# Column logits by a VectorE turn and DMA, chunked first weights, and a recalibrated schedule in a four-layer graph network

## The chip, the cores and the metric

The kernel runs on one core of a Trainium2 chip. The metric is the device time of one execution in microseconds, and the kernel before takes 3336.84 us, the median of three runs (3336.81 to 3337.57). The engines are named as in the profile: PE is TensorE's matrix multiplication and PEld its weight load, DVE is VectorE, ACT is ScalarE, POOL is GpSimd, and SP is the engine whose queue issues every DMA of this kernel.

## The reference, cut to what matters

There are 128 batches, each a graph of 128 nodes with 512 features in float32, and one adjacency matrix for all of them. Four layers follow one another, each with a residual sum and a layer norm:

```python
x = ln(x + (adj @ x) @ W0 + bias0)                        # layer 0
h = x @ W                                                 # layer 1
s1, s2 = h @ a1, h @ a2
e = leaky_relu(s1[:, :, None] + s2[:, None, :], 0.2) * adj
h_prime = softmax(e, axis=2) @ h
x = ln(x + elu(h_prime + beta * h))
x = ln(x + max over n of relu(adj @ x + ...))             # layer 2, a maximum
qkv = x @ w_qkv                                           # layer 3: 8 heads of 64
attn = softmax(where(adj == 0, -inf, q @ k.T * scale))
o = (attn @ v) @ w_proj + b_proj
x = ln(x + o + ln(o) * gamma + beta)
```

In layer 1 the logit of nodes n and m is the sum of a row logit `s1[n]` and a column logit `s2[m]`. The row logits stand one per partition, as a column of a tile. The column logits are wanted along the free axis, the same in every partition, so they have to be turned.

## The kernel before, in words

Every batch is a tile x of 128 partitions (nodes) by 512 features that stays in on-chip memory from its load to its store; there are 16 such buffers. Two batches form a group (`G = 2`). A batch's chain of work is the generator `batch(i)`. Layer 0 mixes nodes with the transposed adjacency (`mixed`, L207) and multiplies by W0 (`product`, L199). The logits s1 and s2 are two reductions on DVE against `wa_rows` (L548), which are W times a1 and a2. For the group's two batches together, `attention1` forms the logits' matrix, the softmax and its transposed form eT, with a round trip through DRAM (`e_d`). Layer 1 mixes with eT, multiplies by W (L199), and applies the ELU on ACT and DVE (L564 to L567). Layer 2 is one matmul (L575), a maximum (L578) and a bias on ACT. Layer 3 turns x by 32x32 blocks on DVE and a round trip through DRAM (`x_d`, to the tile xT), makes queries and keys for the group (`query_key`, L451), values (`values`), the scores (L604), the softmax (L611 to L629), its turn through DRAM (`p_d`, to the tile prT), the weighted sum (`attend`, L480) and the projection (L199 again), with the last two layer norms on DVE. A float32 matmul of the program is two instructions in the trace, a transpose on PE is one.

In `attention1` before, the column logits are turned on PE: L392 transposes a broadcast of the column s2 against the identity, once for each batch of the pair, into a `tr` bank of PSUM, where all partitions then hold s2 along the free axis. L396 reads it from PSUM, in the order of 32-node blocks that the later turn wants, and adds s1 of the partition, twice, into z. L403 to L409 make the leaky maximum, the product with the adjacency and the negated row maximum.

The order of instructions on every engine is written by a planner at build time. `Plan` holds the time at which each engine and each buffer comes free. A chain asks for an engine with `use(engine, work, buffers, late, urgent)`: `work` is how long the engine is held, `late` how long after that the result is there. The request with the earliest start is issued next; among equal starts, urgent ones go first, then the lower rank, which is the batch number. Requests of PE start `MARGIN`, 1.0 us, after their operands. Each engine then runs its instructions strictly in that order, and waits where an operand is late. DMAs are requests on SP, and `landing` estimates when the first loads land. The last six batches have ranks lowered by 12, so that they go ahead of those before them. The buffers that matter here are three PSUM banks `tr`, three `mm`, and 16 buffers x. A buffer is asked for where its name stands in `use`, and `give` frees it.

Work on PE takes these costs in the plan: 3.5 for each product and each query-key block, 0.98 for a mixing, 0.95 for layer 2, 1.1 for scores, 0.25 and 0.9 for each batch's weighted sum, and 0.3 for the logits' transposes.

Of the kernel before, what the change touches and what calls it, by code (L numbers as in the profile page):

```python
# [8 lines left out]
F32 = mybir.dt.float32  # L9
# [6 lines left out]
P = 128  # L16
# [13 lines left out]
    "tr": 3, "mm": 3, "sc": 1,  # L30
    "x": 16, "yT": 3, "e": 2, "et": 1, "eT": 2, "ex": 2, "xT": 2, "v": 8, "qkT": 3,
    "pr": 2, "pt": 1, "xt": 2, "prT": 2, "oT": 2, "o": 2,
# [10 lines left out]
class Plan:  # L43
# [46 lines left out]
    def at(self, r):  # L90
        engine, _, take, _, _ = r["want"]
        t = max(r["ready"] + (MARGIN if engine == "PE" else 0.0), self.free.get(engine, 0.0))
        names = take()
        for n, name in enumerate(names):
            i = (self.next[name] + names[:n].count(name)) % BUFS[name]
            t = max(t, self.slots[name][i])
        return t
# [21 lines left out]
def gnn_stack_kernel(  # L119
# [41 lines left out]
    def mean_rstd(src):  # L161

        yield use("DVE", 1.0)
        st = small.tile([P, 6], F32, name="st")
        nc.vector.bn_stats(st, src)  # L165
        mv = small.tile([P, 2], F32, name="mv")
        nc.vector.bn_aggr(mv, st)  # L167
        ve = small.tile([P, 1], F32, name="ve")
        nc.vector.tensor_scalar(ve, mv[:, 1:2], EPS, None, op0=ALU.add)  # L169
        yield use("POOL", 0.65, late=0.1, urgent=True)  # L170
        rstd = small.tile([P, 1], F32, name="rstd")
        nc.gpsimd.tensor_tensor(rstd, ve, neghalf, op=ALU.pow)  # L172
        return mv, rstd
# [14 lines left out]
    def pool_add(dst, other, event, after=None):  # L188
        if after:
            yield after  # L190
        yield use("POOL", 1.35)
        nc.gpsimd.tensor_tensor(dst, dst, other, op=ALU.add)  # L192
        done(event)
# [8 lines left out]
    def mixed(xb, nodes):  # L202

        b0, b1 = yield use("PE", 0.98, lambda: ("tr", "yT"), late=0.2)
        p = bank([P, K, P], "tr")
        for k in range(K):
            nc.tensor.matmul(p[:, k, :], xb[:, k * P : (k + 1) * P], nodes, start=True, stop=True)  # L207
# [39 lines left out]
    loaded = [Event() for _ in range(NB)]  # L247
    adj_in, adj_ready, w0_in, bias0_in, w1_in = (Event() for _ in range(5))
    scalars_in, w3_in, wa_ready = (Event() for _ in range(3))
# [7 lines left out]
    def load(i):  # L257
        x_slot[i] = yield use("SP", 0.1, "x")
        xs[i] = buf([P, D], "x")
        nc.sync.dma_start(xs[i], x[i])  # L260
        landing(loaded[i], P)
# [4 lines left out]
    def loads():  # L266
# [3 lines left out]
        yield from load(0)  # L270
        yield use("SP", 0.4)
        matrix(w0_sb, w0)
        landing(w0_in, K * P)
        yield from load(1)
# [32 lines left out]

    def adjacency():
        yield adj_in
        b0 = yield use("PE", 0.3, "tr", late=0.2, urgent=True)  # L310
# [41 lines left out]
    class Group:  # L352


        def __init__(self):
            self.s = small.tile([P, G, 2], F32, name="s")
            self.logits = [Event(2) for _ in range(G // 2)]
            self.attention = [Event() for _ in range(G // 2)]
            self.turned, self.qk = Event(G), Event(K)
            self.rows, self.attended = ([Event() for _ in range(G)] for _ in range(2))  # L360
            self.heads, self.o = {}, {}
            self.eT, self.xT, self.qkT, self.slot, self.left = {}, None, None, {}, {}
# [9 lines left out]
    def group(g):  # L372
        if g not in groups:
            groups[g] = Group()
            for h in range(G // 2):
                plan.start(attention1(groups[g], h), g * G + 2 * h - (12 if g * G >= NB - 6 else 0))
            for n in range(K):
                plan.start(query_key(groups[g], n // 2 * 2 + K * (n % 2)), g * G + n / K - (12 if g * G >= NB - 6 else 0))

            for bs in ((0, 1),) if g * G < NB - G else ((0,), (1,)):  # L380
                plan.start(attend(groups[g], bs), g * G - (12 if g * G >= NB - 6 else 0))
        return groups[g]


    def attention1(gr, h):
        yield gr.logits[h]
        yield scalars_in
        s = gr.s
        b0 = yield use("PE", 0.3, "tr", late=0.2, urgent=True)
        p = bank([P, 2, P], "tr")  # L390
        for i in range(2):
            nc.tensor.transpose(p[:, i, :], s[:, 2 * h + i, 1:2].to_broadcast([P, P]), ident)  # L392
        be = yield use("DVE", 2.1, "e", urgent=True)
        z = one.tile([P, 2, P], F32, name="z")
        for i in range(2):
            nc.vector.tensor_scalar(  # L396
                z[:, i, :].rearrange("p (c r) -> p c r", c=Q),
                p[:, i, :].rearrange("p (r c) -> p c r", c=Q),
                s[:, 2 * h + i, 0:1], None, op0=ALU.add,
            )  # L400
        give(b0)
        e = buf([P, 2, P], "e")
        nc.vector.scalar_tensor_tensor(e, z, ALPHA, z, op0=ALU.mult, op1=ALU.max)  # L403
        nc.vector.tensor_tensor(
            e, e, adj_cols.rearrange("p c r -> p (c r)")[:, None, :].to_broadcast([P, 2, P]),
# [22 lines left out]
        scratch = dram.tile([P, Q, 2 * S], F32, name="e_d")  # L428
        yield use("SP", 0.1, late=2.0)
        to_rows(et.rearrange("p c i s -> p c (i s)"), scratch)  # L430
        give(bt)
        gr.slot[h] = yield use("SP", 0.1, "eT", late=2.6)
        eT = buf([P, Q, 2 * S], "eT")
# [5 lines left out]
    def query_key(gr, c):  # L439
        yield gr.turned  # L440
        yield w3_in
        got = yield use("PE", 3.5, lambda: ("mm",) if gr.qkT else ("mm", "qkT"), late=0.2)
        if gr.qkT is None:
# [24 lines left out]
    def attend(gr, bs):  # L468
        for b in bs:
            yield gr.rows[b]  # L470
        slots = yield use(
            "PE", 0.25 + 0.9 * len(bs), lambda: ("tr", "oT") * len(bs), late=0.2, urgent=True
        )
# [17 lines left out]
    def values(i, gr, event):  # L491
        b = i % G
        yield gr.turned
        bp = yield use("PE", 3.5, "mm", late=0.2)
        p = product(
# [10 lines left out]
    def features(xt, bt, gr, b):  # L506

        scratch = dram.tile([P, Q, P], F32, name="x_d", bufs=8)
        yield use("SP", 0.1, late=2.3)
        to_rows(xt, scratch)  # L510
# [13 lines left out]
    def batch(i):  # L524
# [9 lines left out]
        plan.start(pool_add(xb, bias0_sb, biased, bias0_in), i)  # L534
        yield w0_in
        bp = yield use("PE", 3.5, "mm", late=0.2)
        p = product(lambda k: yT[:, k, :], lambda k: w0_sb[:, k, :])
# [6 lines left out]
        yield wa_ready  # L544
        yield use("DVE", 1.6)
        for j in range(2):
# [10 lines left out]
        gr.read(h, 2)  # L557
        bp = yield use("PE", 3.5, "mm", late=0.2)
        p = product(lambda k: yT[:, k, :], lambda k: w1_sb[:, k, :])
# [4 lines left out]
        nc.scalar.activation(ex, p, AF.Exp)  # L564
        yield use("DVE", 1.5, urgent=True)
        nc.vector.scalar_tensor_tensor(xb, p, 0.0, xb, op0=ALU.max, op1=ALU.add)  # L566
# [8 lines left out]
        nc.tensor.matmul(p, adjT, xb, start=True, stop=True)  # L575
# [9 lines left out]

        bt = yield use("DVE", 0.65, "xt")
        xt = buf([P, Q, P], "xt")
# [9 lines left out]

        bs = yield use("PE", 1.1, "sc", late=0.2, urgent=True)
        sc = bank([P, 2, K, P], "sc")
# [54 lines left out]

        bp = yield use("PE", 3.5, "mm", late=0.2)
        p = product(lambda k: oT[:, k, :], lambda k: wproj_sb[:, k, :])
# [9 lines left out]
        yield added  # L666
        yield use("DVE", 1.65)
        t1 = one.tile([P, D], F32, name="t1")
# [5 lines left out]
        yield from layernorm_dve(xb)  # L674
        yield use("SP", 0.1, late=3.0)
        nc.sync.dma_start(out[i], xb)
        give(x_slot[i])

    with tc.manual_schedule(
# [4 lines left out]
        for i in range(NB):  # L684

            plan.start(batch(i), i if i < NB - 6 else i - 12)
        plan.run()
# [27 lines left out]
```

## Time and profile before

| what | value |
|---|---|
| median of three runs | 3336.84 us |
| the profiled execution | 3337.14 us, span 3335.1 us |
| PE busy | 3303.4 us, 99% of the span |
| DVE busy | 2662.2 us, 80% |
| ACT, POOL busy | 1185.1 us (36%), 922.5 us (28%) |
| granted TensorE clock, mean | 0.998 |
| DMA | 296 MB, mean 89 GB/s |

The profile is of one execution. Its own time is 2.0 us over its span, and 0.3 us over the median of the runs. In the rows of groups the columns are: line, engine, operation, what is written and read, shapes, count, then busy us and mean ns of one, then the idle time of the engine just before them and what ended most of it. The names of tiles stand without numbers, so `w_sb` is the weight of layer 0 or of layer 1, `mm` a PSUM bank. PE's matmuls overlap in the array, and so the mean of one (594 ns for 512 columns) is longer than the distance of one start from the next.

### The profile page before, as it was taken

The page shows a single profiled execution, that of the slowest core. Times are in us where ns is not written, and L with a number is a line of the kernel's source. Part 1 is how long each engine was busy: PE and PEld are TensorE (multiplying, and loading weights), DVE is VectorE, ACT ScalarE, POOL GpSimd, SP SyncE. Part 2 cuts the span into 40 slices and gives each one's busy share as a digit, 9 for nine tenths or more (in the row PEclk, how much of TensorE's full clock was granted, in tenths as well). Part 3 has the DMA queues.
Part 4 walks back from the last instruction along what each step waited for, and adds up shares of the span by engine and source line. Part 5 has one row for each costly group of instructions (what it writes and reads, how often), then busy time and mean ns, then how long its engine had stood idle before and what let it go on. Part 6 is the DMA issues. An engine that isn't in the chain of part 4 may idle for free.

```text
span 3335.1 us, 43586 instructions
## 1 busy us (share of the span) xinstructions
PE 3303.4 (99%) x14729; PEld 2069.6 (62%) x14729; DVE 2662.2 (80%) x5527; ACT 1185.1 (36%) x3457; POOL 922.5 (28%) x1031
## 2 busy tenths in 40 slices
PE   9999999999999999999999999999999999999998
PEld 5666666566656666656566666556666656656655
DVE  7878779877878778877986877987787877887786
ACT  3433333333334343333343333234233333334332
POOL 2222223222232322312331322412232232332232
PEclk9999999999999999999999999999999999999999
DMA  4322322232222222232223223223322223222232
GB/s 159 100 97 69 98 89 59 97 99 92 86 89 71 91 92 86 77 107 82 74 82 113 81 83 89 83 89 83 111 79 86 73 94 97 72 86 81 74 105 78
DMA packets 458190, 296.00 MB, mean 89 GB/s; under 512 B 315888, under 2 KB 389744, under 8 KB 457968
## 3 DMA queue, kind: packets, MB, share of 16 engines
q1 hardware_dynamic: 457968, 293.23, 28.9%
q8 instruction: 117, 1.92, 0.2%
q14 instruction: 105, 0.86, 0.1%
HBM read 150.54 MB, written 142.61 MB: 88 GB/s over the span
## 4 chain that ended last, share of the span: by engine, by line
PE 87%; DVE 11%; DMA 1%; issue 1%; SPq 0%; ACT 0%; POOL 0%; POOLq 0%; DVEq 0%
PE mm L199 45%; PE mm L451 25%; PE tr L207 5%; PE sc L604 4%; PE tr L480 3%; PE mm L575 3%; DVE st L165 2%; DVE scr L548 1%; DVE x L186 1%; DVE x L541 1%; DVE mv L167 1%; DVE xt L588 1%; DVE x L672 0%; DVE mx L578 0%; DVE x L567 0%
## 5 line engine op out<-in xcount | busy, mean ns | idle before, releaser
L199 PE MATMUL mm<-w_sb,yT 128*128 128x512 f32 x2048 | 910.7, 594 | 1.7 <-DVE x L566 1.2
L451 PE MATMUL mm<-xT,wqkv_sb 128*128 128x256 f32 x4096 | 908.0, 380 | 1.0 <-DVE mx L578 1.0
L451 PEld LDWEIGHTS mm<-xT,wqkv_sb 128*128 128x128 f32 x4096 | 772.5, 190 | 130.1 <-issue 18.8
L172 POOL TENSOR_TENSOR rstd<-ve,neghalf 128x1 f32<-128x1 f32 x640 | 407.6, 637 | 1461.7 <-DVE ve L169 1232.8
L199 PEld LDWEIGHTS mm<-w_sb,yT 128*128 128x128 f32 x2048 | 381.0, 190 | 444.9 <-issue 431.3
L199 PE MATMUL mm<-wqkv_sb,xT 128*128 128x512 f32 x1024 | 464.3, 596 | 0.0
L622 ACT ACTIVATE pr<-pr,nmx 128x128 f32<-128x128 f32 x1024 | 397.7, 391 | 170.0 <-DVE nmx L618 168.6
L199 PE MATMUL mm<-wproj_sb,oT 128*128 128x512 f32 x1024 | 457.0, 595 | 0.0
L192 POOL TENSOR_TENSOR x<-x,o 128x512 f32<-128x512 f32 x128 | 177.2, 1385 | 659.9 <-DVE o L660 658.0
L165 DVE BATCH_NORM_STATS2 st<-x 128x6 f32<-128x512 f32 x512 | 349.0, 682 | 8.1 <-ACT x L582 7.3
L199 PEld LDWEIGHTS mm<-wproj_sb,oT 128*128 128x128 f32 x1024 | 192.6, 191 | 226.2 <-issue 222.9
L181 ACT ACTIVATE x<-x,nmr,rstd 128x512 f32<-128x512 f32 x256 | 205.1, 810 | 338.7 <-DVE nmr L179 314.2
L199 PEld LDWEIGHTS mm<-wqkv_sb,xT 128*128 128x128 f32 x1024 | 188.4, 190 | 197.4 <-issue 190.7
L611 DVE TENSOR_TENSOR pr<-sc,maskb 128x1024 f32<-128x1024 f32 x128 | 156.0, 1219 | 189.6 <-PE sc L604 189.5
L210 ACT COPY yT<-tr 128x512 f32<-128x512 f32 x256 | 147.9, 583 | 232.6 <-PE tr L207 232.2
L192 POOL TENSOR_TENSOR x<-x,bias_sb 128x512 f32<-128x512 f32 x128 | 178.4, 1402 | 129.4 <-PE tr L207 121.3
L192 POOL TENSOR_TENSOR x<-x,beta_sb 128x512 f32<-128x512 f32 x128 | 167.3, 1309 | 157.5 <-DVE xt L588 142.0
L548 DVE SCALAR_TENSOR_TENSOR scr<-x,wa_rows 128x512 f32<-128x512 f32 x256 | 192.2, 751 | 17.8 <-ACT x L181 11.9
L459 ACT ACTIVATE qkT<-mm 128x512 f32<-128x512 f32 x128 | 76.0, 593 | 339.0 <-PE mm L451 338.8
L622 ACT ACTIVATION_READ_ACCUMULATOR pr<-pr,nmx 128x1 f32 x1024 | 193.3, 189 | 0.0
L500 ACT COPY v<-mm 128x512 f32<-128x512 f32 x128 | 74.8, 585 | 333.0 <-PE mm L199 333.0
L186 DVE TENSOR_SCALAR x<-x,mv,rstd 128x512 f32<-128x512 f32 x256 | 168.1, 661 | 14.4 <-POOL rstd L172 14.3
(63 smaller groups left out, 3551.2 us busy)
## 6 DMA issues: line engine op xcount, KB each, us to landing
p_d<-pt SPq DMA_DIRECT2D x128, 512.0 KB, 2.6
prT<-p_d SPq DMA_DIRECT2D x128, 512.0 KB, 3.8
x<-in_x SPq DMA_DIRECT2D x128, 256.0 KB, 2.7
x_d<-xt SPq DMA_DIRECT2D x128, 256.0 KB, 2.0
xT<-x_d SPq DMA_DIRECT2D x512, 64.0 KB, 2.4
out<-x SPq DMA_DIRECT2D x128, 256.0 KB, 2.0
e_d<-et SPq DMA_DIRECT2D x64, 128.0 KB, 1.7
eT<-e_d SPq DMA_DIRECT2D x64, 128.0 KB, 2.2
```

The lines of the kernel that those rows point to most:

```text
L165: nc.vector.bn_stats(st, src)
L172: nc.gpsimd.tensor_tensor(rstd, ve, neghalf, op=ALU.pow)
L181: nc.scalar.activation(xb, xb, AF.Identity, bias=nmr, scale=rstd)
L186: nc.vector.tensor_scalar(xb, xb, mv[:, 0:1], rstd, op0=ALU.subtract, op1=ALU.mult)
L192: nc.gpsimd.tensor_tensor(dst, dst, other, op=ALU.add)
L199: nc.tensor.matmul(p, lhs(k), rhs(k), start=(k == 0), stop=(k == K - 1))
L207: nc.tensor.matmul(p[:, k, :], xb[:, k * P : (k + 1) * P], nodes, start=True, stop=True)
L210: nc.scalar.copy(yT, p)
L451: nc.tensor.matmul(p[:, j, :], wqkv_sb[:, k, (c + j) * P : (c + j + 1) * P], gr.xT[:, k, :], start=(k == 0), stop=(k == K - 1),)
L548: nc.vector.scalar_tensor_tensor(scr, xb, 1.0, wa_rows[:, j, :], op0=ALU.mult, op1=ALU.mult, accum_out=gr.s[:, b, j : j + 1],)
L611: nc.vector.tensor_tensor(pr, sc.rearrange("p j c m -> p (j c) m"), maskb[:, None, :].to_broadcast([P, H, P]), op=ALU.add,)
L622: nc.scalar.activation(pr[:, j, :], pr[:, j, :], AF.Exp, bias=nmx[:, j : j + 1], accum_out=sums[:, j : j + 1],)
```

## The change

The column logits no longer go through PE. DVE turns a broadcast of s2 by 32x32 blocks into the small tile s2 (64 elements per partition, both batches of the pair). One DMA writes four partitions of it, one of each block of 32 nodes, to DRAM (`s_d`) in the order of 32-node blocks that z has, and a second reads that row of 256 numbers into all 128 partitions of the tile z. One addition of 128x256 on DVE then adds s1. The reads wait on SP's queue for the write's landing.

The first weights come as four DMAs of 128 rows instead of one, and batch 0's first product is planned on the second chunk. Twelve transposes of the identity stand on PE ahead of the adjacency's transpose; nothing reads them. `MARGIN` counts for a request only in proportion to its ready time up to 20 us of plan. Many planned durations change; the ELU's second step and layer 2's second step on DVE become requests of their own, and their PSUM banks are given free before them. The last eight batches have ranks lowered by 8, instead of the last six by 12. The scratch rows p_d have eight buffers instead of four, and a group takes both its prT buffers at once.

```diff
-    "x": 16, "yT": 3, "e": 2, "et": 1, "eT": 2, "ex": 2, "xT": 2, "v": 8, "qkT": 3,
+    "x": 16, "yT": 3, "z": 2, "e": 2, "et": 1, "eT": 2, "ex": 2, "xT": 2, "v": 8, "qkT": 3,
...
-        t = max(r["ready"] + (MARGIN if engine == "PE" else 0.0), self.free.get(engine, 0.0))
+        t = max(r["ready"] + (min(MARGIN, r["ready"] / 20) if engine == "PE" else 0.0), self.free.get(engine, 0.0))
...
-        yield use("DVE", 1.0)
+        yield use("DVE", 1.03)
         st = small.tile([P, 6], F32, name="st")
...
-        yield use("POOL", 1.35)
+        yield use("POOL", 1.4)
         nc.gpsimd.tensor_tensor(dst, dst, other, op=ALU.add)
...
-        b0, b1 = yield use("PE", 0.98, lambda: ("tr", "yT"), late=0.2)
+        b0, b1 = yield use("PE", 0.91, lambda: ("tr", "yT"), late=0.2)
...
-        x_slot[i] = yield use("SP", 0.1, "x")
+        x_slot[i] = yield use("SP", 0.5, "x")
...
-        yield use("SP", 0.4)
-        matrix(w0_sb, w0)
-        landing(w0_in, K * P)
+        for k in range(K):
+            yield use("SP", 0.4)
+            nc.sync.dma_start(w0_sb[:, k, :], w0[k * P : (k + 1) * P])
+            landing(w0_chunk[k], P)
         yield from load(1)
...
     def adjacency():
+
+        b0 = yield use("PE", 2.5, "tr")
+        p = bank([P, K, P], "tr")
+        for i in range(12):
+            nc.tensor.transpose(p[:, i % K, :], ident, ident)
+        give(b0)
         yield adj_in
...
-                plan.start(attention1(groups[g], h), g * G + 2 * h - (12 if g * G >= NB - 6 else 0))
+                plan.start(attention1(groups[g], h), g * G + 2 * h - (8 if g * G >= NB - 8 else 0))
...
         s = gr.s
-        b0 = yield use("PE", 0.3, "tr", late=0.2, urgent=True)
-        p = bank([P, 2, P], "tr")
-        for i in range(2):
-            nc.tensor.transpose(p[:, i, :], s[:, 2 * h + i, 1:2].to_broadcast([P, P]), ident)
+
+        yield use("DVE", 0.2)
+        st = small.tile([P, 2, Q, S // Q], F32, name="s2")
+        nc.vector.transpose(
+            st.rearrange("p i c u -> p i u c"),
+            s[:, 2 * h : 2 * h + 2, 1:2, None].to_broadcast([P, 2, S // Q, Q]),
+        )
+        row = dram.tile([2 * Q, Q, S // Q], F32, name="s_d")
+        yield use("SP", 0.5, late=2.0)
+        nc.sync.dma_start(
+            row.rearrange("j a u -> a j u"), st[::S].rearrange("p i c u -> p (i c) u")
+        )
+        bz = yield use("SP", 0.5, "z", late=2.2)
+        z = buf([P, 2, P], "z")
+        nc.sync.dma_start(
+            z, row.rearrange("j a u -> (j a u)")[None, :].to_broadcast([P, 2 * P]).rearrange(
+                "p (i f) -> p i f", i=2
+            ),
+        )
         be = yield use("DVE", 2.1, "e", urgent=True)
-        z = one.tile([P, 2, P], F32, name="z")
-        for i in range(2):
-            nc.vector.tensor_scalar(
-                z[:, i, :].rearrange("p (c r) -> p c r", c=Q),
-                p[:, i, :].rearrange("p (r c) -> p c r", c=Q),
-                s[:, 2 * h + i, 0:1], None, op0=ALU.add,
-            )
-        give(b0)
+        nc.vector.tensor_tensor(
+            z, z, s[:, 2 * h : 2 * h + 2, 0:1].to_broadcast([P, 2, P]), op=ALU.add
+        )
         e = buf([P, 2, P], "e")
         nc.vector.scalar_tensor_tensor(e, z, ALPHA, z, op0=ALU.mult, op1=ALU.max)
+        give(bz)
...
-        got = yield use("PE", 3.5, lambda: ("mm",) if gr.qkT else ("mm", "qkT"), late=0.2)
+        got = yield use("PE", 3.46, lambda: ("mm",) if gr.qkT else ("mm", "qkT"), late=0.2)
...
-        yield w0_in
-        bp = yield use("PE", 3.5, "mm", late=0.2)
+        yield w0_chunk[1]
+        bp = yield use("PE", 3.46, "mm", late=0.2)
...
-        yield use("DVE", 1.6)
+        yield use("DVE", 1.7)
         for j in range(2):
...
-        yield use("DVE", 1.5, urgent=True)
+        yield use("DVE", 0.69, urgent=True)
         nc.vector.scalar_tensor_tensor(xb, p, 0.0, xb, op0=ALU.max, op1=ALU.add)
+        give(bp)
+        yield use("DVE", 0.8)
         nc.vector.scalar_tensor_tensor(xb, ex, 1.0, xb, op0=ALU.min, op1=ALU.add)
-        give(bp)
         give(be)
...
-        bp = yield use("PE", 0.95, "mm", late=0.2, urgent=True)
+        bp = yield use("PE", 0.88, "mm", late=0.2, urgent=True)
...
-        yield use("DVE", 0.89, urgent=True)
+        yield use("DVE", 0.69, urgent=True)
         mx = small.tile([P, 1], F32, name="mx")
         nc.vector.tensor_reduce(mx, p, axis=AX.X, op=ALU.max)
+        give(bp)
+        yield use("DVE", 0.21)
         nc.vector.tensor_scalar(mx, mx, b2_sb, 0.0, op0=ALU.add, op1=ALU.max)
-        give(bp)
...
-        bs = yield use("PE", 1.1, "sc", late=0.2, urgent=True)
+        bs = yield use("PE", 1.13, "sc", late=0.2, urgent=True)
...
-        scratch = dram.tile([P, Q, H * S], F32, name="p_d")
-        yield use("SP", 0.1, late=2.8)
+        scratch = dram.tile([P, Q, H * S], F32, name="p_d", bufs=8)
+        yield use("SP", 0.5, late=2.8)
         to_rows(pt.rearrange("p c h s -> p c (h s)"), scratch)
         give(bt)
-        bt = yield use("SP", 0.1, "prT", late=4.0)
+        got = yield use("SP", 0.5, lambda: () if gr.prT else ("prT",) * G, late=4.0)
+        gr.prT = gr.prT or got
+        bt = gr.prT.pop()
...
-        yield use("DVE", 1.65)
+        yield use("DVE", 1.9)
         t1 = one.tile([P, D], F32, name="t1")
...
-            plan.start(batch(i), i if i < NB - 6 else i - 12)
+            plan.start(batch(i), i if i < NB - 8 else i - 8)
```

More of the change, by code (lines that the diff above doesn't have):

```diff
@@ L247, in gnn_stack_kernel @@
     loaded = [Event() for _ in range(NB)]
-    adj_in, adj_ready, w0_in, bias0_in, w1_in = (Event() for _ in range(5))
+    adj_in, adj_ready, bias0_in, w1_in = (Event() for _ in range(4))
+    w0_chunk = [Event() for _ in range(K)]
     scalars_in, w3_in, wa_ready = (Event() for _ in range(3))
@@ L360, in __init__ @@
             self.rows, self.attended = ([Event() for _ in range(G)] for _ in range(2))
-            self.heads, self.o = {}, {}
+            self.heads, self.o, self.prT = {}, {}, []
             self.eT, self.xT, self.qkT, self.slot, self.left = {}, None, None, {}, {}
@@ L375, in group @@
             for h in range(G // 2):
-                plan.start(attention1(groups[g], h), g * G + 2 * h - (12 if g * G >= NB - 6 else 0))
+                plan.start(attention1(groups[g], h), g * G + 2 * h - (8 if g * G >= NB - 8 else 0))
             for n in range(K):
-                plan.start(query_key(groups[g], n // 2 * 2 + K * (n % 2)), g * G + n / K - (12 if g * G >= NB - 6 else 0))
+                plan.start(query_key(groups[g], n // 2 * 2 + K * (n % 2)), g * G + n / K - (8 if g * G >= NB - 8 else 0))
             for bs in ((0, 1),) if g * G < NB - G else ((0,), (1,)):
-                plan.start(attend(groups[g], bs), g * G - (12 if g * G >= NB - 6 else 0))
+                plan.start(attend(groups[g], bs), g * G - (8 if g * G >= NB - 8 else 0))
         return groups[g]
@@ L428, in attention1 @@
         scratch = dram.tile([P, Q, 2 * S], F32, name="e_d")
-        yield use("SP", 0.1, late=2.0)
+        yield use("SP", 0.5, late=2.0)
         to_rows(et.rearrange("p c i s -> p c (i s)"), scratch)
         give(bt)
-        gr.slot[h] = yield use("SP", 0.1, "eT", late=2.6)
+        gr.slot[h] = yield use("SP", 0.5, "eT", late=2.6)
         eT = buf([P, Q, 2 * S], "eT")
@@ L471, in attend @@
         slots = yield use(
-            "PE", 0.25 + 0.9 * len(bs), lambda: ("tr", "oT") * len(bs), late=0.2, urgent=True
+            "PE", 0.25 + 0.88 * len(bs), lambda: ("tr", "oT") * len(bs), late=0.2, urgent=True
         )
@@ L508, in features @@
         scratch = dram.tile([P, Q, P], F32, name="x_d", bufs=8)
-        yield use("SP", 0.1, late=2.3)
+        yield use("SP", 0.5, late=2.3)
         to_rows(xt, scratch)
@@ L534, in batch @@
         plan.start(pool_add(xb, bias0_sb, biased, bias0_in), i)
-        yield w0_in
-        bp = yield use("PE", 3.5, "mm", late=0.2)
+        yield w0_chunk[1]
+        bp = yield use("PE", 3.46, "mm", late=0.2)
         p = product(lambda k: yT[:, k, :], lambda k: w0_sb[:, k, :])
@@ L557, in batch @@
         gr.read(h, 2)
-        bp = yield use("PE", 3.5, "mm", late=0.2)
+        bp = yield use("PE", 3.46, "mm", late=0.2)
         p = product(lambda k: yT[:, k, :], lambda k: w1_sb[:, k, :])
@@ L583, in batch @@
         yield from layernorm_dve(xb)
-        bt = yield use("DVE", 0.65, "xt")
+        bt = yield use("DVE", 0.71, "xt")
         xt = buf([P, Q, P], "xt")
@@ L653, in batch @@
         give(ba)
-        bp = yield use("PE", 3.5, "mm", late=0.2)
+        bp = yield use("PE", 3.46, "mm", late=0.2)
         p = product(lambda k: oT[:, k, :], lambda k: wproj_sb[:, k, :])
@@ L674, in batch @@
         yield from layernorm_dve(xb)
-        yield use("SP", 0.1, late=3.0)
+        yield use("SP", 0.5, late=3.0)
         nc.sync.dma_start(out[i], xb)
```

## The prediction

> **What bounds the kernel now.** I read the page first: busy time, then the groups by line with shapes kept apart, then PE's waits, then the chain and the timeline at both ends.
>
> ```profile
> span 3335.1 us, 43586 instructions
> ...
> PE 3303.4 (99%) x14729; PEld 2069.6 (62%) x14729; DVE 2662.2 (80%) x5527; ACT 1185.1 (36%) x3457; POOL 922.5 (28%) x1031
> ```
>
> TensorE (PE) is busy 99% of the span and is idle for 3335.1 - 3303.4 = 31.7 us in all. The next engine, VectorE (DVE), has a fifth of its time free. So a change gains only by taking instructions off PE or by closing PE's 31.7 us. The waits of PE say where those are (columns: total us, times, longest):
>
> ```profile
> PE tr L392 <- DVE scr L548: 6.2, 8, 1.2
> PE tr L480 <- DMA prT<-p_d: 4.4, 2, 4.1
> PE tr L207 <- DMA x<-in_x: 3.3, 2, 2.3
> PE tr L312 <- DMA adj_sb<-in_adj: 2.6, 1, 2.6
> PE mm L575 <- ACT x L181: 1.4, 2, 0.7
> PE mm L199 <- DVE x L566: 1.2, 1, 1.2
> ```
>
> The largest is in front of the very transposes that the change removes. About 10 us more lie after the last matmul. The chain of waits gives PE's pace:
>
> ```profile
> 70.11 0.22 PE tr L392 x2
> ```
> ```profile
> 283.87 0.32 PE tr L392
> ```
> ```profile
> 3213.22 17.17 PE mm L199 x40
> ```
>
> The two logit transposes of a pair of batches take 0.22 us when nothing is late, 0.11 each; 40 matmuls of 512 columns take 17.17, so a product of eight takes 3.43. The piece at 283.87 is one transpose that had waited for the logits' reductions on DVE. PE's timeline at the start and at the end:
>
> ```profile
> 4.10 2.04 PE L207 MATMUL tr<-adjT,x 128*128 128x128 f32 x8 [1.02 <-DMA x<-in_x]
> 8.41 2.07 PE L207 MATMUL tr<-adjT,x 128*128 128x128 f32 x8 [2.27 <-DMA x<-in_x]
> 10.28 7.68 PE L199 MATMUL mm<-w_sb,yT 128*128 128x512 f32 x16
> ```
> ```profile
> 3309.03 1.09 PE L480 MATMUL tr<-prT,v 128*64 128x128 f32 x16
> 3314.26 1.97 PE L480 MATMUL tr<-prT,v 128*64 128x128 f32 x16 [4.13 <-DMA prT<-p_d]
> 3316.16 8.57 PE L199 MATMUL mm<-wproj_sb,oT 128*128 128x512 f32 x16
> ```
>
> At the start, the first product stands behind the mixing of batch 1, which waits for that batch's x. At the end the attention of the last batch waits 4.1 us for its DMA, while the projection of the batch before, whose operand was copied at 3310.8, stands behind it; after that idle time the granted clock is 0.59 (windows of 5 us, 3315 to 3320), and 16 matmuls take 8.57 us instead of 6.9.
>
> **The change part by part**, against the profiled execution: span 3335.1, with 2.0 around it 3337.1; the median of the runs, 3336.8, is 0.3 lower.
>
> *Transposes off PE.* 64 pairs of 0.22 us: -14.1 us. All of it is on the path, since PE is the bound there.
>
> *The wait in front of them.* PE's idle time there is 6.2 us by the waits, PEld's 9.7; counted from matmul start to matmul start in the trace, the places at L392 hold 9.4 us more than 0.11 for each. It goes, but DVE was late there, and the next matmul fed by DVE may wait instead. At 283.87 independent matmuls follow for 6.9 us, so most of it does not come back: bounds 0 and -9.4, I take -7.5.
>
> *What VectorE gets instead.*
>
> ```profile
> L396 DVE TENSOR_SCALAR z<-tr,s 128x128 f32<-128x128 f32 x128 | 38.5, 342 | 3.1 <-PE tr L392 3.0
> L404 DVE TENSOR_TENSOR e<-e,adj_cols 128x256 f32<-128x256 f32 x64 | 31.0, 484 | 2.2
> L426 DVE STREAM_TRANSPOSE et<-e 128x128 f32<-128x128 f32 x128 | 39.9, 311 | 5.1 <-DMA e_d<-et 0.8
> ```
>
> Two adds from PSUM go (38.5 us in all). One add of 128x256 comes, like L404, 0.48, and one block transpose of 128x64, between the smallest DVE operation (0.15, L169) and L426's 0.31: I take 0.22, from its half size. 64 x 0.70 = 45 us, so DVE gains 6 us of work and stays at 80%: nothing on PE's path.
>
> *Two more DMAs per pair on SP's queue.* Nearest rows, in us to landing:
>
> ```profile
> e_d<-et SPq DMA_DIRECT2D x64, 128.0 KB, 1.7
> eT<-e_d SPq DMA_DIRECT2D x64, 128.0 KB, 2.2
> ```
>
> Their issues take 0.33 and 0.37, so 128 more cost SP's queue about 45 us of 3335, beside everything else. Round trip: 1.7 + 2.2 = 3.9, up to 3.2 + 3.9 = 7.1 by the longest of each. The plan allows 0.5 + 2.0 + 0.5 + 2.2 = 5.2, so there is 1.3 us of slack, and PE's requests are planned 1.0 us behind their operands besides. The new wait is of DVE: the add at the head of a pair's 2.1 us of work. Behind it stand evacuations of PSUM (L541, L566, L660) for which PE waits by the three mm banks. On SP, the read holds whatever is queued behind it (x loads, p_d, x_d) until the write has landed, as p_d does now (265.5 us in 112 waits of SP). Bounds 0 and +54 us (below, the second rival); nearest are the medians: +1. The batch's longer latency is covered by 16 x buffers, 16 x 26 us of work.
>
> *First weights in chunks, dummy transposes.* w0 lands at 1.65 + 6.04 = 7.7 and the first product starts at 10.28. With chunks it is planned on the second chunk and hence ahead of batch 1's mixing. The dummies start when the identity is there (1.3) and take 12 x 0.22 (the mixing's pace at the start) = 2.6, to 3.95; adjacency's transpose 0.44 and copy 0.29, mixing to 6.6, its copy 0.59: product at 7.3. At full pace it ends at 10.8, and with batch 1's mixing and product at 15.5 to 16, against 17.79 now. If the array stays slow until 11.6, as it does now (from there the trace's clock record is 1.0), five matmuls take 0.85 each (start to start of the first product's first ones now) and the second product ends near 17.3. Bounds -3 and +1 (the dummies delay adjacency by 1.3); I take -1.5. The four issues of 0.43 move x1, bias and w1 back by 1.3 us on SP, behind 327 GB/s of transfers in the first 20 us, which is what they land by.
>
> The Trainium skill, "TensorE: Matmul & The Clock Gate", Part 4 on PE-mode transposes, says that transposes do not count as activity that raises the clock. By it the dummies would raise nothing, the start would bring 0.5 and the sum would be 3311; no run here shows it yet.
>
> *Calibrated plan.* From the planner's costs a batch asked 26.2 us of PE before (4 products and 2 query-key blocks at 3.5, two mixings at 0.98, 0.95, 1.1, about 1.2 for the rest) and 25.6 now; the chain shows 25.3. So PE ran ahead of the plan, relative to DVE, whose costs rise (a batch from 22.1 to 22.8; busy 20.8). Other waits of PE in mid-kernel sum to some 5 to 6 us from start to start (L575, L451 and L199 behind ACT and DVE). A truer plan should close some; a new order can open others: bounds -6 and +8, I take -2. SP's 0.5 for 0.1 (0.33 to 0.37 measured) moves requests apart in the plan; SP's planned 5.5 us per batch stay far under 25. Twice the p_d buffers and the paired prT cost nothing: SP's waits name no p_d reader, and attention frees both prT at once now.
>
> *Last eight ahead by 8 instead of six by 12.* It changes the filler work behind the last softmax. The order named above costs 4.1 idle and 1.7 of slow clock. Best -8 (both, and some of the 10 us after the last matmul), worst +8 (less filler: the last softmax to prT takes 3296.3 to 3314.1, and 12.2 of these 17.8 us are filled now). I take -3, half of what the misplaced projection costs.
>
> Sum: -14.1 - 7.5 + 1 - 1.5 - 2 - 3 = -27.1: 3310.0, by the median's offset 3309.7, rounded 3310.
>
> The skill's "VectorE: DVE Perf Modes", Rules for kernel authors, gives 128x128 transposes to TensorE where PSUM will do. That speaks against the change: by it nothing is gained and the time stays near 3337. The rule takes PE to have room, and this trace has PE at 99% against DVE at 80%.
>
> **Rivals.**
> 1. *The waits only move.* DVE was late, not the transposes; the next matmul pays, and ends and plan bring nothing net: 3337.1 - 14.1 and the start's 1.5 = 3321.5. For it: PEld waits 4.7 us in 9 places at L575 behind ACT too. Against it: independent matmuls follow.
> 2. *The logits' round trip holds VectorE* (slower). If each takes the longest rows, 7.1, DVE waits 1.9 beyond the plan, 0.9 beyond PE's margin, 64 x 0.85 = 54 us: 3310 + 54 = 3364. It decides from 0.4 us of PE wait per pair, a round trip of 6.6. Against it: medians of 3.9.
> 3. *The rebuilt order gives it back*: the plan's and the tail's worst bounds, +8 and +8, in place of -2 and -3, and 4 us of waits at the round trip: 3310 + 10 + 11 + 4 = 3335, no change. For it: the tail's filler is tight. Against it: PE's pace in the plan comes nearer to the chain's.
> 4. *Everything closes*: -14.1 - 9.4 - 3 - 6 - 8 = 3296.5, about 3297.
>
> **How the numbers follow.** Forecast 0.62 (3300 to 3320), rival 1 0.19, rival 2 0.07, rival 3 0.06, rival 4 0.06. 0.2% or 6.7 us is about what a measurement of this kernel tells from no change. Faster: 0.62 + 0.19 + 0.06 = 0.87; same 0.06; slower 0.07. The range 3299 to 3328 takes in rival 1 with some of a bad tail and leaves out rivals 2 and 3 and most of 4, nearly 0.2.
>
> **What would show it.** L392 gone and PE with 128 fewer matmuls; span down by 14 plus what PE's idle time falls, from 31.7 to about 19; DVE's idle in front of the new add under 10 us in total (rival 2: over 50); the first product at 7 to 8 us, at a pace that tells whether the dummies raised the clock; the last two projections not behind a wait of 4 us. The prediction is wrong if PE's idle grows at L575, L207 (eT) or L480, or if the tail after 3300 is longer.

## The result, and the profile after

The changed kernel takes 3312.35 us, the median of four runs (3311.0 to 3316.2), against 3337.03 before: a ratio of 0.9928, with a 95% interval of 0.9910 to 0.9945. The forecast was 3310. The total was right. Four of the six terms it was summed from were not: the wait and the plan by errors that cancel, the start and the tail. The experiments below show it.

The page of the changed kernel, its span and its first line of busy times:

```profile
span 3309.2 us, 43603 instructions
...
PE 3286.0 (99%) x14613; PEld 2060.0 (62%) x14613; DVE 2640.0 (80%) x5527; ACT 1182.6 (36%) x3457; POOL 935.1 (28%) x1031
```

The span is 25.9 us shorter. PE has 116 matmuls fewer: the 128 logit transposes are gone and the twelve dummies have come. PE is idle for 3309.2 - 3286.0 = 23.2 us instead of 31.7; 19 was forecast. DVE is no busier than before.

The windows view cuts the span into the start, the middle and the end. Its columns are: the stretch and its length, then busy us and instructions of PE, PEld, DVE, ACT and POOL, then granted clock, DMA share and GB/s. First the kernel before, then the one after:

```profile
0.00:60.00 60.00, 51.98 (x200) 30.73 (x201) 42.69 (x108) 15.11 (x29) 21.50 (x26) 1.00 0.58 211
60.00:3050.00 2990.00, 2980.81 (x13294) 1867.83 (x13293) 2407.32 (x5014) 1078.35 (x3143) 831.45 (x928) 1.00 0.29 86
3050.00:3336.00 286.00, 270.57 (x1237) 171.09 (x1235) 212.15 (x406) 91.66 (x286) 69.58 (x79) 0.98 0.28 86
```
```profile
0.00:60.00 60.00, 57.58 (x222) 33.93 (x223) 42.51 (x102) 15.86 (x29) 23.43 (x27) 1.00 0.56 207
60.00:3050.00 2990.00, 2987.25 (x13301) 1877.10 (x13300) 2406.11 (x5067) 1082.65 (x3158) 845.83 (x931) 1.00 0.30 90
3050.00:3310.00 260.00, 241.19 (x1094) 148.97 (x1092) 191.36 (x360) 84.13 (x271) 65.83 (x73) 0.97 0.29 89
```

Length less busy time is PE's idle time, the last stretch taken to the end of the span:

| stretch | before | after |
|---|---|---|
| 0 to 60 us | 8.0 | 2.4 |
| 60 to 3050 us | 9.2 | 2.8 |
| 3050 us to the end | 14.5 | 18.0 |

The middle and the start gained, the end lost. In the start, 2.8 us of the busy time after are the dummies, which do no work. Counted from matmul starts at the pace of full clock, PE has done its first 40 us of real work at 52 us before and at 47 after, so the start gains about 5 us.

PE's waits of the changed kernel (total us, times, longest; line numbers have moved, so attention is L499 here and layer 2 is L595):

```profile
PE tr L499 <- DMA prT<-p_d: 4.6, 1, 4.6
PE mm L595 <- ACT x L181: 2.1, 1, 2.1
PE mm L199 <- ACT yT L210: 2.0, 2, 1.4
PE mm L199 <- ACT oT L675: 1.5, 2, 0.7
```

The wait behind the logits' reductions (6.2) is gone. The wait for the last prT (4.4 before) is still there: it is the same wait one batch earlier, as PE's timeline at the end shows:

```profile
3272.60 1.16 PE L625 MATMUL sc<-qkT 64*128 64x128 f32 x16
3273.69 7.13 PE L199 MATMUL mm<-wproj_sb,oT 128*128 128x512 f32 x16
3285.42 1.44 PE L499 MATMUL tr<-prT,v 128*64 128x128 f32 x16 [4.60 <-DMA prT<-p_d]
3287.59 6.30 PE L199 MATMUL mm<-wproj_sb,oT 128*128 128x512 f32 x8 [0.73 <-ACT oT L675]
3293.82 1.09 PE L499 MATMUL tr<-prT,v 128*64 128x128 f32 x16
3295.66 3.70 PE L199 MATMUL mm<-wproj_sb,oT 128*128 128x512 f32 x8 [0.74 <-ACT oT L675]
```

The last two batches now go in the order attention, projection, attention, projection, so no projection stands behind another batch's wait. But PE runs out of work at 3280.8, waits at the attention of the last batch but one, and the eight matmuls after that take 6.3 us instead of 3.7; the trace's clock record is 0.5 from 3286.0 to 3292.9.

### The profile page after: what moved, and what is told of

Same layout as the page of the kernel before. It is cut to its first block, busy times and chain, and to the rows that moved or that the text cites. A ratio compares the mean times of both kernels' runs of the same rounds, so it can differ in the third digit from the quotient of the medians.

```text
span 3309.2 us, 43603 instructions
## 1 busy us (share of the span) xinstructions
PE 3286.0 (99%) x14613; PEld 2060.0 (62%) x14613; DVE 2640.0 (80%) x5527; ACT 1182.6 (36%) x3457; POOL 935.1 (28%) x1031
## 4 chain that ended last, share of the span: by engine, by line
PE 97%; DVE 2%; DMA 1%; issue 0%; POOL 0%; ACT 0%; SPq 0%; POOLq 0%; ACTq 0%; DVEq 0%
PE mm L199 52%; PE mm L470 27%; PE tr L207 7%; PE sc L625 4%; PE tr L499 4%; PE mm L595 3%; DVE e L442 0%; DMA z<-s_d 0%; DVE st L165 0%; DVE scr L567 0%; DVE x L560 0%; DVE x L186 0%; DMA prT<-p_d 0%; DVE et L445 0%; PE tr L315 0%
## 5 line engine op out<-in xcount | busy, mean ns | idle before, releaser
L172 POOL TENSOR_TENSOR rstd<-ve,neghalf 128x1 f32<-128x1 f32 x640 | 418.2, 654 | 1528.5 <-DVE ve L169 1241.9
L632 DVE TENSOR_TENSOR pr<-sc,maskb 128x1024 f32<-128x1024 f32 x128 | 156.2, 1220 | 156.1 <-PE sc L625 155.8
L625 PEld LDWEIGHTS sc<-qkT 64*128 64x128 f32 x2048 | 124.2, 187 | 81.9 <-issue 65.0
```

The costliest lines, as they stand in the source:

```text
L625: nc.tensor.matmul(sc[:, j, c, :], gr.qkT[rws, c, nodes], gr.qkT[rws, K + c, nodes], start=True, stop=True,)
L632: nc.vector.tensor_tensor(pr, sc.rearrange("p j c m -> p (j c) m"), maskb[:, None, :].to_broadcast([P, H, P]), op=ALU.add,)
```

## The experiments

Every run is set against the kernel before on the same chip. "Idle in the middle" is PE's, between 60 and 3050 us, by the windows view. The runs were on several chips, on which the kernel before takes 3337.03 to 3337.87 us, so a difference of under 1 us to the changed kernel says nothing.

**The round trip alone, in the plan of before.**

```diff
 (the kernel before)
-    "x": 16, "yT": 3, "e": 2,
+    "x": 16, "yT": 3, "z": 2, "e": 2,
...
 (attention1: the two transposes and the additions from PSUM
  replaced by the turn, the two DMAs and the one addition)
```

> The kernel before with one part of the change alone: the column logits by VectorE's turn and the two DMAs, with the z buffers; every other cost, rank and the start are those of before. Theory (PE's work and the waits in front of it both go): 3337 - 14.1 - 6 = 3317, up to 5 us either way from the new order. Rival, the waits only move: 3337 - 14.1 = 3323, with as much PE idle time behind ACT and DVE as the 6 to 9 us at the transposes before. Rival, the round trip holds VectorE and PE with it: above 3330.

3328.34 us (3325.27 to 3331.76), 0.9973 of before [0.9963, 0.9983]. It gains 8.8 us where I expected 20. The middle and PE's waits of this run:

```profile
60.00:3050.00 2990.00, 2977.67 (x13242) 1865.47 (x13241) 2421.55 (x5037) 1085.70 (x3152) 845.19 (x930) 1.00 0.30 90
```
```profile
PE mm L586 <- ACT x L181: 4.0, 3, 2.2
PE tr L207 <- DMA eT<-e_d: 3.3, 4, 1.2
...
PE sc L615 <- DVE pr L622: 2.4, 3, 1.0
PE mm L462 <- DVE mx L589: 1.6, 1, 1.6
```

The idle time of the middle is 12.3 us, more than the 9.2 with the transposes. The waits in front of the transposes are gone, but as much idle time and more now stands at layer 2, at the mixing with eT and at the scores. That is what rival 1 says. The order is a new one in this run, and eT comes after the round trip, so how much of this is the old lateness passed on is not told apart.

**The transposes back, in the changed plan.**

```diff
 (the changed kernel)
 (attention1: turn, two DMAs and addition replaced by)
+        b0 = yield use("PE", 0.3, "tr", late=0.2, urgent=True)
+        p = bank([P, 2, P], "tr")
+        for i in range(2):
+            nc.tensor.transpose(p[:, i, :], s[:, 2 * h + i, 1:2].to_broadcast([P, P]), ident)
...
```

> The changed kernel with the two PE transposes and the additions from PSUM back in the place of the round trip; start, costs and ranks as changed. Theory: 3312 + 14.1 of PE work + 3 to 6 of waits behind the logits' reductions = 3330, the tail up to 8 either way. If the gain came from the calibrated plan and the ends and not from PE's work: 3318 or less.

3330.68 us (3330.36 to 3333.04), 0.9981 [0.9971, 0.9990]. The sum came out as expected; its parts did not. The idle time of the middle is 2990 - 2988.18 = 1.8 us, with the transposes in place, and of PE's waits only the last one here is at them:

```profile
60.00:3050.00 2990.00, 2988.18 (x13365) 1879.89 (x13365) 2403.10 (x5035) 1079.57 (x3148) 840.75 (x925) 1.00 0.29 87
```
```profile
PE tr L488 <- DMA prT<-p_d: 10.6, 1, 10.6
...
PE tr L400 <- DVE scr L556: 0.8, 1, 0.8
```

The other 4 us or so are the tail, where the attention of the last group waits 10.6 us for its prT instead of 4.6. So the changed plan closes the wait in front of the transposes without removing them.

**The same work on PE, waiting for nothing.**

```diff
 (the changed kernel, layer 2)
         p = bank([P, D], "mm")
+        if b == 0:
+            for n in range(2):
+                nc.tensor.transpose(p[:, :P], ident, ident)
         nc.tensor.matmul(p, adjT, xb, start=True, stop=True)
```

> The changed kernel with two transposes of the identity per pair of batches in front of layer 2's matmul, in the same PSUM bank, which that matmul then overwrites: 0.22 us of PE work per pair that waits for nothing new, with the plan's order unchanged. Theory (all PE work is on the path): 3312.4 + 14.1 = 3326.5. If PE had room that the busy share hides: 3312 to 3317.

3325.61 us (3323.94 to 3326.16), 13.3 more than the changed kernel. 64 x 0.22 = 14.1 us of work costs nearly its full length even where it waits for nothing: PE has no room. This is the term of the sum that was sure, and it holds.

**No dummies at the start.**

```diff
 (the changed kernel, adjacency)
-        b0 = yield use("PE", 2.5, "tr")
-        p = bank([P, K, P], "tr")
-        for i in range(12):
-            nc.tensor.transpose(p[:, i % K, :], ident, ident)
-        give(b0)
```

> The changed kernel without the twelve transposes of the identity at the start; the order of everything else is unchanged. If the dummies raise the clock: adjacency's transpose at 2.6, mixing at 4.1 in 2.0 us as before, first product at 6.7 with its first four or five matmuls 0.85 apart, the second product ending 1 to 2 us later than with dummies; 3313.5, hardly told from 3312.4. If transposes do not count as activity: the first product at the pace it has with them (3.70 for eight), and the time 0.5 to 1 us shorter, 3311.5.

3314.41 us (3312.11 to 3315.09); the times alone do not tell it from 3312.35. PE's timeline does. First the run without dummies, then the changed kernel:

```profile
4.00 2.05 PE L207 MATMUL tr<-adjT,x 128*128 128x128 f32 x8 [0.86 <-DMA x<-in_x]
6.72 6.68 PE L199 MATMUL mm<-w_sb,yT 128*128 128x512 f32 x8 [0.68 <-ACT yT L210]
13.24 2.84 PE L207 MATMUL tr<-adjT,x 128*128 128x128 f32 x24
```
```profile
1.36 2.82 PE L315 MATMUL tr<-ident 128*128 128x128 f32 x12 [1.36 <-POOL ident masks.py:199]
3.97 0.42 PE L320 MATMUL tr<-ident,adj_sb 128*128 128x128 f32 x1
4.78 1.64 PE L207 MATMUL tr<-adjT,x 128*128 128x128 f32 x8 [0.39 <-DVE adjT L322]
7.09 3.70 PE L199 MATMUL mm<-w_sb,yT 128*128 128x512 f32 x8 [0.68 <-ACT yT L210]
10.63 2.84 PE L207 MATMUL tr<-adjT,x 128*128 128x128 f32 x24
```

Without dummies the product starts 0.4 us sooner and takes 6.68 us, all of it at the slow pace; with them it takes 3.70. PE is at the next mixing 2.6 us sooner. The clock records agree: full clock begins at 5.8 us after and at 12.7 here. So in this execution the dummies do what they are for. In two other profiles that have them, the same work on PE and the durations of before, the full clock begins at 4.2 and 4.6 us, when PE had run nothing but transposes; the first mixing then runs at full pace, 1.16 us instead of 2.05. PE's timeline with the same work on PE:

```profile
1.36 2.82 PE L315 MATMUL tr<-ident 128*128 128x128 f32 x12 [1.36 <-POOL ident masks.py:199]
3.97 0.40 PE L320 MATMUL tr<-ident,adj_sb 128*128 128x128 f32 x1
4.76 1.16 PE L207 MATMUL tr<-adjT,x 128*128 128x128 f32 x8 [0.38 <-DVE adjT L322]
```

The Trainium skill, "TensorE: Matmul & The Clock Gate", Part 4 on PE-mode transposes, says that the full clock does not engage for transposes, which do not count as busy in the same way; these runs show that twelve of them, in float32, did raise it.

**The ranks of before.**

```diff
 (the changed kernel)
-            plan.start(batch(i), i if i < NB - 8 else i - 8)
+            plan.start(batch(i), i if i < NB - 6 else i - 12)
 (and so for attention1, query_key and attend)
```

> The changed kernel with the ranks of before: the last six batches ahead by 12, not the last eight by 8. The order differs only where the last batches are loaded and after. Theory (ranks set how much PE work is left to fill the last softmax): the time up to 3200 is unchanged, the last 100 us grow by 3 to 8: 3316 to 3320. If the ranks do nothing for the tail, as the profile after suggests (9.5 us of PE waits after 3269 against 6.7 before): 3312, or less.

3315.57 us (3312.63 to 3316.03). The runs overlap those of the changed kernel, so the ranks' part is not told apart by time. Its profile has PE waiting 5.6 us for prT in two places instead of 4.6 in one. What "last eight ahead" brought is a few us at most. PE is idle 3314.3 - 3050 - 244.26 = 20.0 us after 3050 us, against 18.0 with the changed ranks and 14.5 before. So the longer idle time of the tail does not come from the ranks.

**The durations of before, in the changed kernel.**

```diff
 (the changed kernel; PE, DVE and POOL costs as before, SP's outside the new round trip)
-        bp = yield use("PE", 3.46, "mm", late=0.2)
+        bp = yield use("PE", 3.5, "mm", late=0.2)
...
-        yield use("SP", 0.5, late=2.8)
+        yield use("SP", 0.1, late=2.8)
```

> The changed kernel planned with the durations of before (PE 3.5, 0.98, 0.95, 1.1, 0.9; DVE 1.0, 1.6, 1.65, 0.65; POOL 1.35; SP 0.1 outside the new round trip); instructions, start and ranks as changed. Theory, after the run that put the round trip into the plan of before: the calibrated durations and not the missing transposes close PE's waits in mid-kernel, so waits over 0.2 us between 60 us and the tail rise from 5.6 to 12 to 19 us, and the time to 3320 to 3330. Rival, the durations don't matter and the round trip closed them: 3312 to 3316.

3323.36 us (3321.58 to 3324.87), 0.9958 [0.9943, 0.9973]. The time is in the expected range, though not by the expected way. Idle in the middle is 2990 - 2984.72 = 5.3 us, twice that of the changed kernel, but waits over 0.2 us sum to 6.8 from 60 to 3050 us, short of the 12 to 19 expected. More than half of the 11 us are in the tail: PE waits 10.7 us for the last prT, and is idle 3321.3 - 3050 - 247.14 = 24.2 us after 3050 us, against 18.0.

```profile
60.00:3050.00 2990.00, 2984.72 (x13253) 1873.33 (x13253) 2415.29 (x5061) 1083.87 (x3159) 846.58 (x930) 1.00 0.30 90
```

**The changed durations, in the kernel before.**

```diff
 (the kernel before; PE, DVE, POOL and SP costs as changed, nothing else)
-        yield use("DVE", 1.0)
+        yield use("DVE", 1.03)
...
-        b0, b1 = yield use("PE", 0.98, lambda: ("tr", "yT"), late=0.2)
+        b0, b1 = yield use("PE", 0.91, lambda: ("tr", "yT"), late=0.2)
...
```

> The kernel before, with its PE transposes, its start and its ranks, planned with the changed durations and nothing else of the change. Read between 60 and 3050 us, where PE is idle 9.2 us before, 12.3 with the round trip alone, 2.8 after. Theory (the durations close PE's waits in mid-kernel, with or without the transposes): 2 to 4 us idle there. If the durations need the earlier release of the banks or the missing transposes: 7 to 10. The whole time follows the tail that the old ranks make with this plan, whose own times have 39 us of gaps of PE in the last 100: 3335 to 3360.

3352.55 us (3351.43 to 3353.54), 1.0044 [1.0027, 1.0061]: slower than before. The middle, and PE's waits:

```profile
60.00:3050.00 2990.00, 2987.66 (x13380) 1879.44 (x13380) 2411.82 (x5007) 1080.47 (x3163) 832.41 (x921) 1.00 0.29 87
```
```profile
PE tr L480 <- DMA prT<-p_d: 15.9, 2, 12.7
PE mm L575 <- ACT x L181: 11.4, 2, 10.9
...
PE tr L392 <- DVE scr L548: 1.1, 2, 0.5
```

Here the middle and the end stand apart. The durations alone take the idle time of the middle from 9.2 to 2.3 us, and the wait at the transposes from 6.2 to 1.1, while the transposes are still there. And the same new order, with the old ranks, has a tail with 16 us of waits for prT and 11 more at layer 2. In these runs the truer plan helps where work is plenty. It does not settle the end: with the same old ranks PE is idle after 3050 us for 14.5 us before, for 38.3 here, and for 20.0 with the whole rest of the change.

**The round trip planned 4 us too short.**

```diff
 (the changed kernel, attention1)
-        yield use("SP", 0.5, late=2.0)
+        yield use("SP", 0.5, late=0.0)
...
-        bz = yield use("SP", 0.5, "z", late=2.2)
+        bz = yield use("SP", 0.5, "z", late=0.2)
```

> The changed kernel with the round trip planned 4.0 us too short (0.5 + 0.0 + 0.5 + 0.2), so that the addition stands in VectorE's order before z has landed. Rival 2's mechanism put to the test at a size of its own: z comes some 3 us later than planned, 64 times. If a wait of VectorE beyond PE's margin of 1.0 us passes to PE in full: 64 x 2 = 130 us, 3440. If VectorE's idle fifth takes it up: VectorE's wait at the addition grows from 31 to 150 us or more, and the time stays under 3325. I expect between: a third passed on, 3355.

3379.88 us (3374.06 to 3384.06), 1.0126 [1.0111, 1.0141]: 67.5 us over the changed kernel. DVE's wait at the addition, first here, then in the changed kernel:

```profile
DVE z L417 <- DMA z<-s_d: 191.1, 63, 6.6
```
```profile
DVE z L417 <- DMA z<-s_d: 31.4, 24, 4.9
```

VectorE waits 160 us more, 2.5 per pair, and the kernel pays 67.5, or 42%. Rival 2's mechanism exists: a late z stops DVE with everything behind it, and PE then waits at the scores (18.0 us behind L632) and elsewhere. More than half was taken up, by DVE's idle fifth or by PE's margin in the plan; the run does not tell which. My bound had let all of it through beyond PE's margin. In the profiled execution PE is idle 71.6 us instead of 23.2; the other 18 us of the longer span are the same 14613 instructions of PE taking longer (busy 3303.7 us instead of 3286.0), with a mean granted clock of 0.994 instead of 0.998. In the changed kernel the 31.4 us of such waits leave little at PE: idle in the middle is 2.8 us, and 1.8 with the transposes back.

**The last twelve batches ahead by six.**

```diff
 (the changed kernel)
-            plan.start(batch(i), i if i < NB - 8 else i - 8)
+            plan.start(batch(i), i if i < NB - 12 else i - 6)
 (and so for attention1, query_key and attend)
```

> The changed kernel with the last twelve batches ahead by 6. In the planner's own times the longest gap of PE at the end, 6.8 us in front of the attention of batch 126, becomes 2.0 and the plan ends 11.6 us earlier. Theory (the tail follows the plan): PE's wait of 4.6 us for prT and the slow clock behind it go, and the time is 3302 to 3306. If the tail is set by what the plan does not know: 3312.

3301.55 us (3300.84 to 3303.09), 0.9893 [0.9878, 0.9908]. This beats both kernels: its interval lies below that of the changed kernel, by 10.8 us in the medians. PE's timeline at its end:

```profile
3269.13 1.97 PE L499 MATMUL tr<-prT,v 128*64 128x128 f32 x32
3271.12 7.13 PE L199 MATMUL mm<-wproj_sb,oT 128*128 128x512 f32 x16
3278.19 1.09 PE L499 MATMUL tr<-prT,v 128*64 128x128 f32 x16
3280.02 3.70 PE L199 MATMUL mm<-wproj_sb,oT 128*128 128x512 f32 x8 [0.74 <-ACT oT L675]
3283.65 1.09 PE L499 MATMUL tr<-prT,v 128*64 128x128 f32 x16
3285.49 3.70 PE L199 MATMUL mm<-wproj_sb,oT 128*128 128x512 f32 x8 [0.74 <-ACT oT L675]
```

No wait for prT is left, and the last projections run at full clock, 3.70 each. The numbers were picked by the planner's own times for PE's gaps, which end 11.6 us sooner with them.

**The last ten by six, with a smaller margin.**

```diff
-MARGIN = 1.0
+MARGIN = 0.85
...
-            plan.start(batch(i), i if i < NB - 8 else i - 8)
+            plan.start(batch(i), i if i < NB - 10 else i - 6)
```

> The changed kernel with the last ten batches ahead by 6 and a margin of 0.85 instead of 1.0 for PE's requests; the plan's own times end 3.3 us before those of twelve by six. If the chip follows the plan that closely: 3297 to 3300. If what is left is start, end and matmul starts 0.1 us late that no wait explains: 3301.5 as with twelve by six, within 1.5.

3303.71 us (3303.43 to 3303.96): 2.2 us slower than twelve by six, where the plan has it 3.3 sooner. The chip is another one, on which the kernel before takes 0.5 us more, and the intervals of the two ratios overlap; it is not faster, at any rate. The plan's times told a tail of 7 us of gaps from one of 2. They did not tell these 3 us.

## Why the prediction was right, and where its steps were not

*Transposes off PE, -14.1.* Right: the same work put back costs 13.3 us.

*The wait in front of them, -7.5, and the calibrated plan, -2.* The sum, 9.5, is near what the middle gave: 6.4 us less idle time, and 8.5 less in waits over 0.2 us counted from matmul start to matmul start (11.9 to 3.4). The step that failed is "It goes, but DVE was late there, and the next matmul fed by DVE may wait instead ... most of it does not come back". As much idle time and more stood elsewhere as long as the plan was the old one (12.3 us idle with the round trip alone). What closed it are the durations (2.3 us idle with the durations alone). Leaving out the round trip planned short, every profile with the changed durations has 1.8 to 2.8 us there, with and without the transposes, and the three with the old ones have 5.3, 9.2 and 12.3. So rival 1 was right that the transposes' going does not close it, and the sum was saved by a term that I had priced at 2. Between the round trip in the old kernel (12.3) and the changed kernel with the old durations (5.3), another 7 us went with the rest of the change; whether through the banks given free sooner, the start or the chance of an order was not separated.

*What VectorE gets.* Right: the turn takes 0.28 us instead of my 0.22 and the addition 0.47 instead of 0.48; DVE stays at 80%.

*Two more DMAs, +1.* The price at PE was about right, the size of the wait was not: I expected under 10 us of DVE's idle time at the addition, and it is 31.4. The term mis-sized is the round trip, "1.7 + 2.2 = 3.9". Where the addition stood waiting, in the run planned short, write issue to read issue takes 1.68 and read issue to addition 2.93; from the turn's end to the addition it is 4.8 (all medians). The row eT<-e_d that I took for the read was to the landing, 2.2; to the use it is about as long as z's: where PE waited for eT (ten places in six profiles), it started 2.4 to 3.5 us after the issue. In the changed kernel the read also stood in SP's queue: 1.72 to the read's issue in the median, up to 7.7. (By rival 2's own figures its price is 64 x 0.9 = 58, not 64 x 0.85 = 54.)

*The start, -1.5.* Mis-sized: about -5. The dummies bring 2.6 in the profiled execution, so the clock came as in the better case that I had worked out: the first product ends at 10.8, as I had it there. I had left out that the two longest waits at the transposes up to 60 us, 1.2 and 0.8 us at 38 and 58 us, belong to the start as well (the 5 us have the first of them). The pace of 0.85 that I read from "the first product's first ones" rested on one matmul start to the next, the second was 0.65; the run without dummies has five in a row at 0.85.

*The tail, -3.* The wrong way: +3.5 us of idle time. The step that failed is "half of what the misplaced projection costs". The projection was put in its place, but the wait of 4.6 us is now at the batch before, since the filler ran out, which stood in the sentence before as the worst bound. The term also put the whole change of the tail down to the ranks. With the ranks of before the changed kernel's tail is idle no less (20.0 against 18.0), so the loss came with the rest of the new order; which part of it made the tail longer was not separated. With twelve by six the tail is idle 3299.1 - 3050 - 237.68 = 11.4 us, 3.1 less than before.

By its own signs the prediction was off in more places than its total shows: 23.2 us of idle time instead of 19, 31.4 at the addition instead of under 10, a wait of 4.6 us left at the end. PE's idle time also grew, which was to say that the prediction is wrong, at layer 2 (1.4 to 2.1), at the mixing with eT (none to 0.4) and at the attention (4.4 to 4.6); that is 1.3 us in all.

The parts as measured, -14.1 of work, -8.5 in the middle, -5 at the start and +3.5 at the end, make -24.1 against the -24.7 of the medians. So 3310 against 3312 is partly luck: the start gave 3.5 us more than its term, the tail 6.5 less. The rule "VectorE: DVE Perf Modes" of the Trainium skill, Rules for kernel authors, to transpose 128x128 on TensorE where PSUM will do, was weighed against PE's 99% and left; the 13.3 us that 64 pairs of transposes cost here are the number for that.

## What to carry to other kernels

Where one engine is busy 99% of the span, work taken off it can be worth its length, and that can be measured by putting the same work back with no wait; taken off alone, in the old plan, it brought 8.8 of 14.1 us here. A wait in front of an instruction need not go with the instruction: if the schedule has the producer late, another reader may wait; correct the schedule's durations and look at the middle of the span and at its end apart. The end needs a choice of its own: here the order of the last twelve batches was worth 10.8 us, more than the middle gained.

## What the runs showed of the hardware that was not expected

- Float32 transposes on PE raised the clock. In the eight profiles with the dummies full clock begins at 4.2 to 6.2 us in six and at 10.6 to 10.8 in two; in the four without them (before, the round trip alone, no dummies, the durations alone) at 11.6 to 14.4. The two late ones (transposes back; ranks of before) had a first product of 5.2 to 5.3 us instead of 3.7, so the same program can differ by 2 us at its start. The dummies' own pace is 0.21 us from start to start, as in the first mixing without them (0.21); at full clock it is 0.11.
- From 157 to 176 times between 60 and 3050 us, in every profile, a matmul starts about 0.105 us late with no wait and no operand behind it. That is 16 to 18 us in each kernel, after this change more than all other idle time of the middle. In the changed kernel each of the 162 is the second instruction of a group of eight (of a product, a query-key block or a mixing) or of layer 2's two, and the run without dummies, with the same order, has them at the same 162 places. So they go with the order and not with chance. It was not tried what they are.
